# Cross-attention block: two query tiles' scores in one block, one ring of PSUM banks, exchanges gated by target, layer norms placed anew

## Chip, cores and metric

One core of one Trainium2 chip runs the whole kernel in one launch. The metric is the device time in microseconds (us) of that launch; lower is better. TensorE (PE) multiplies, VectorE (DVE) and ScalarE (ACT) work on its results, GpSimd (POOL) does small element work, and SyncE (SP) issues nearly all transfers from one in-order queue.

## What is computed

All in float32, for 4 batches of 512 queries and 512 keys, width 512, 16 heads of 32, inner width 2048:

```python
y = layer_norm(x) * ln1_w + ln1_b
q, k, v = y @ q_w + q_b, ctx @ k_w + k_b, ctx @ v_w + v_b      # 16 heads of 32
attn = softmax(where(mask, q @ k.T / sqrt(32), lowest))        # 512 x 512 per head
hidden = (attn @ v) @ cproj_w + cproj_b + x
z = layer_norm(hidden) * ln2_w + ln2_b
out = hidden + gelu_tanh(z @ fc_w + fc_b) @ proj_w + proj_b
```

## The kernel before

The work has two parts. In the first (to about 551 us) the attention of all batches runs, and the MLP of batch 0 and half of the MLP of batch 1 are filled in between; in the second, `last_mlps`, the rest of the MLPs runs. Instruction order on every engine is the order of the program text (a manual schedule), so each engine is a queue in that order.

The attention is cut into 16 `w` = (batch, group of 4 heads), each with 4 query tiles of 128 (`qt`): 64 units `u = 4w + qt`. Two units make a pair, numbered `2w + half`. One unit does this:

- `scores(w, qt)`: four matmuls, one for each head (L262). A head is only 32 rows deep, so the four lie side by side in four row strips of the array. They write the one tile of the pool `ps_sc`: `[128, 4, 512]`, four PSUM banks, one buffer. The other four banks are the pool `ps_acc`, which all other products take in turn (`acc_tile`).
- Then, head by head, DVE adds the mask and takes the row minimum (L266; the scores are negated), and ACT takes the exponential with its row sum (L270). This is called softening here.
- `turn(w, qt)`: DVE transposes 32 x 32 squares of two heads at a time into the pair's tile `tb` (L285, L293), with the reciprocals of the sums (L290, L292, L294). `tb` has two buffers.
- After a pair's second unit, `exchange()` and `copies` move `tb` across partition strips to the pair's target with 16 DMAs on SP's queue (L328): `pT` (one buffer), or the spare tile `gt` for pairs 1, 3, 5, 7, or `xe` for pairs 25, 27, 29, 31. A pair for `pT` waits in `waiting` while another pair is in `held`, and pairs behind it wait with it.
- `attend(w, half)`: 16 matmuls with four column strips (L345, tile `av`), multiplied by the reciprocals on DVE into `oT` (L350); only then is the target free. The table `AT` and `LAG` say in which unit a pair is attended: as a rule in the first unit of the block after next, at the beginning and the end of the attention in a second unit.

Between `scores` of one unit and the next, PE gets other work, from hand-written lists (`first`, `later`): the key, query and value products of later groups (`prep_k`, `prep_q`, `prep_v`: `acck`, `accq`, `accv`), the output product `cproj` (`accc`, four for a batch), the pairs of MLP products by a seven-product scheme (`fc_seven`, tiles `q...`), plain MLP products (`accf`) and the second MLP product (`accp`). Evictions of these go to ACT (K, Q, V, the copy `p1` and gelu of a pair) or DVE (sums into `h`, the adds of `fc_seven`).

A layer norm is `ln_stat` (DVE, L128 and L129, a tile of 128 rows each), `ln_rs` (POOL, L134 and L136, and two more for keys in `BY_ACT`, L140 and L141), `ln_norm` (DVE L150, or ACT L146 for keys in `BY_ACT`), and `ln_turn` (PE transposes, tile `tp`, scaled by ACT L164 or DVE L162). A key is (1 or 2, batch).

Of the kernel before, what the change touches and what calls it, by code (L numbers as in the profile page):

```python
# [12 lines left out]
F32 = mybir.dt.float32  # L13
# [20 lines left out]
AHEAD = 3  # L34
SPLIT = 1
FIRST = 2
LAG = 4
# [15 lines left out]
def xattn_block(ctx: ExitStack, tc: tile.TileContext, x, encT, mask, q_w, k_w, v_w, c_w, fc_w, p_w, vecs, rows, out):  # L53
# [3 lines left out]
    def pools(stack, **bufs):  # L57
        return [stack.enter_context(tc.tile_pool(name=n, bufs=k)) for n, k in bufs.items()]
# [3 lines left out]
    ps_acc = ctx.enter_context(tc.tile_pool(name="ps_acc", bufs=4, space=PSUM))  # L62
# [3 lines left out]
    ps_sc = att.enter_context(tc.tile_pool(name="ps_sc", bufs=1, space=PSUM))  # L66
# [53 lines left out]
    def acc_tile(name):  # L120
        return ps_acc.tile([P, D], F32, tag="acc", name=name)
# [9 lines left out]
    def ln_rs(key):  # L131

        ve = small.tile([P, NT], F32, tag="ve", name=f"ve{key[0]}_{key[1]}")
        nc.gpsimd.tensor_scalar(ve, S["mv", key][:, :, 1], EPS, 1.0, ALU.add, ALU.mult)  # L134
        rs = small.tile([P, NT], F32, tag="rs", name=f"rs{key[0]}_{key[1]}")
        nc.gpsimd.tensor_tensor(rs, ve, nhalf, ALU.pow)  # L136
        S["rs", key] = rs
        if key in BY_ACT:
            nm = small.tile([P, NT], F32, tag="nm", name=f"nm{key[0]}_{key[1]}")
            nc.gpsimd.tensor_tensor(nm, S["mv", key][:, :, 0], rs, ALU.mult)  # L140
            nc.gpsimd.tensor_scalar(nm, nm, -1.0, 0.0, ALU.mult, ALU.add)  # L141
            S["nm", key] = nm

    def ln_norm(key, t, dst, src):
        if key in BY_ACT:
            nc.scalar.activation(  # L146
                dst, src, AF.Identity, bias=S["nm", key][:, t : t + 1], scale=S["rs", key][:, t : t + 1]
            )
            return
        nc.vector.tensor_scalar(  # L150
            dst, src, S["mv", key][:, t, 0:1], S["rs", key][:, t : t + 1], ALU.subtract, ALU.mult
        )
# [102 lines left out]
    def scores(w, qt):  # L255
        if qt == 0:
            S["sums", w] = small.tile([P, NT, HG], F32, tag="sums", name=f"sums_{w}")
        qT, kT, sums = S["qT", w], S["kT", w], S["sums", w]
        sc = ps_sc.tile([P, HG, L], F32, tag="sc", name=f"sc_{w}_{qt}")
        for h in range(HG):  # L260
            r = slice(h * HD, (h + 1) * HD)
            nc.tensor.matmul(sc[:, h, :], qT[r, ts(qt, P)], kT[r, :], start=True, stop=True)  # L262
        for h in range(HG):
            s = score_tile()
            mn = small.tile([P, 1], F32, tag="mn", name=f"mn_{w}_{qt}_{h}")
            nc.vector.tensor_tensor_reduce(  # L266
                out=s, in0=sc[:, h, :], in1=S["mb", w // NG], scale=1.0, scalar=FMAX,
                op0=ALU.add, op1=ALU.min, accum_out=mn,
            )
            nc.scalar.activation(s, s, AF.Exp, bias=mn, scale=-1.0, accum_out=sums[:, qt, h : h + 1])  # L270
            if h % 2:
                S["ps", w, qt, h // 2] = score_pair()

    def turn(w, qt):

        half, q = divmod(qt, 2)
        if q == 0:


            S["tb", w, half] = two.tile([P, NI, PW + 2 * HD], F32, tag="tb", name=f"tb_{w}_{half}")  # L280
        tb = S["tb", w, half]
        tv = tb[:, :, :PW].rearrange("p j (a t h q) -> p a h t j q", a=2, t=NT, h=HG)
        two_heads = [(tv[:, q, 2 * k : 2 * k + 2], S["ps", w, qt, k]) for k in range(HG // 2)]
        for k in range(HG // 2 - q):
            nc.vector.transpose(*two_heads[k])  # L285
        if q == 0:
# [6 lines left out]
        nc.vector.transpose(*two_heads[-1])  # L293
        nc.vector.transpose(  # L294
            tb[:, :, PW:].rearrange("p j (a q) -> p a j q", a=2), rr.rearrange("p a h d -> p (a h d)")
        )
        waiting.append((w, half))
        if w < NW - 1 or half == 0:
            exchange()

    waiting, held = [], []

    def exchange():

        while waiting:
            w, half = waiting[0]
            if 2 * w + half not in IN_G + IN_XE:
                if held:
                    return
                held.append((w, half))  # L310
            waiting.pop(0)
            copies(w, half)

    def copies(w, half):
        tb = S["tb", w, half]

        pair = 2 * w + half
        if pair in IN_G or pair in IN_XE:
            pT = (gt if pair in IN_G else xe).rearrange("p (i n) -> p i n", i=NI)
        else:  # L320
            pT = one.tile([P, NI, PW + 2 * HD], F32, tag="pT", name=f"pT_{w}_{half}")
# [9 lines left out]
    def attend(w, half):  # L331
# [19 lines left out]
        if (w, half) in held:  # L351
            held.remove((w, half))
# [237 lines left out]
    def last_mlps():  # L590
        last, = pools(ctx, last=1)
        ps_last = ctx.enter_context(tc.tile_pool(name="ps_last", bufs=4, space=PSUM))
# [241 lines left out]
    def do(fn):  # L834
        return [(0.0, fn)]
# [60 lines left out]
    for part in range(3):  # L896
# [15 lines left out]
    first = [[] for _ in range(NW)]  # L912
    later = [[] for _ in range(NW)]
    k2, q2, v2 = A(2)
    k3, q3, v3 = A(3)
    k4, q4, v4 = A(4)
    k5, q5, v5 = A(5)
    k6, q6, v6 = A(6)
    first[0] = (
        [(CHAIN, lambda: prep_v(1))], [v2, k2] + x2[:1], [k3, (CHAIN, lambda: (prep_v(3), load_enc(1)))] + x2[1:2],  # L920
        [(CHAIN, lambda: prep_q(1))]
    )
    first[1] = [q2] + x2[2:], [k4], [v4], [q3]
    first[2] = x3[:2] + [k5], x3[2:], [v5], [q4]
    first[3] = [q5], [k6], [v6], [q6] + do(lambda: c_bias(0))
# [31 lines left out]
    def norm(b, *ts_):  # L957
        return do(lambda: [norm2(b, t) for t in ts_])


# [3 lines left out]
    first[4] = x1 + [k, q, v] + x4  # L964
    later[4] = c[:1] + x2[:1] + c[1:2] + x2[1:2] + c[2:3] + x2[2:] + c[3:]
    k, q, v = A(8)
    first[5] = (
        [k] + stat(0, 0, 1, 2, 3) + rs(0) + do(fc_sums) + x3 + norm(0, 0, 1, 2, 3) + [v], [q] + t2 + do(lambda: y_sums(0)), some(2) + pb_(0), some(2)
    )
    k, q, v = A(9)  # L970
    x1, x2, x3, x4 = inputs(3)
    first[6] = [k, q] + some(4) + [v] + x1
    k, q, v = A(10)
    first[7] = [k, q] + x2[:1] + some(2) + x2[1:2] + some(2) + [v]

    k, q, v = A(11)
    first[8] = h_(1, 0, 1) + x2[2:] + [k, q] + x3[:2] + some(2) + x3[2:3] + [v] + x3[3:] + h_(1, 2, 3) + x4
    later[8] = cb(1) + C(1)
    k, q, v = A(12)
    first[9] = [q] + some(2) + [k] + some(2) + [v]  # L980
    k, q, v = A(13)
    first[10] = [k, q] + some(4) + [v]
    k, q, v = A(14)
    t2 = turns2(1)
    first[11] = (
        [k, q] + stat(1, 0, 1, 2, 3) + rs(1), some(2) + norm(1, 0, 1, 2, 3), some(1) + t2[:2] + [v],
        t2[2:] + pb_(1) + some(1) + h_(2, 2, 3, 0, 1)
    )

    k, q, v = A(15)  # L990
    c = C(2)
    first[12] = [k, q], cb(2) + [v], c[:2], c[2:]
    first[13] = some(1), some(1) + stat(2, 0, 1), some(1) + stat(2, 2, 3) + rs(2), some(2)
    first[14] = some(1) + norm(2, 0, 1), some(1) + norm(2, 2, 3), some(2), some(1)
    first[15] = hid_(1, 2, 3) + some(1), some(1), some(1), some(2)

    for w in range(NW):
        if w and w % NG == 0:
            make_mb(w // NG)

        work, rest = first[w], later[w]
        by_unit = isinstance(work, tuple)
        share = 0 if by_unit else sum(c for c, _ in work + rest) / NT
        due = 0.0
        for qt in range(NT):
            u = w * NT + qt
            pair = AT.get(u, (u - LAG) // 2 if u >= LAG and u % 2 == 0 else None)
            if pair in AT.values() and u not in AT:
                pair = None
            if pair is not None:  # L1010
                attend(*divmod(pair, 2))
            scores(w, qt)
            turn(w, qt)
            if by_unit:
                run(work[qt])
                continue

            if qt == 2:
                work, rest = work + rest, []
            due += share / 2  # L1020
            due -= run(work, due)
            due += share / 2
            due -= run(work, due)
        if not by_unit:
            run(work + rest)
# [5 lines left out]
    run(some(2))  # L1031
    attend(NW - 1, 0)
    run(some(2))
    load_wa(first_c)
    run(some(2))
    p_sums(first_c)
    attend(NW - 1, 1)
    run(mlp)
# [52 lines left out]
```

## Time and profile before

| | |
|---|---|
| time, median of 3 runs | 797.86 us (797.24 to 799.24) |
| span of the profiled execution, first to last instruction | 795.4 us |
| median less that span, which is what lies around the span if the profiled execution was like the median run | 2.4 us |
| busy share of the span: PE, DVE, ACT, POOL | 98%, 78%, 43%, 18% |
| attention part, to the first product of `last_mlps` | about 551 us |
| mean granted TensorE clock | 0.998 |

The profile names instructions by line, engine, operation and tiles (`out<-in`). A float32 matmul leaves two records, a transpose on PE one, so `sc L262 x8` is one unit's four score matmuls. In the chain of waits and in the timeline the first number is the start in us from the span's beginning and the second the length. SP's queue only issues: its rows are the time of issuing, and a transfer lands later.

### The profile page before, as it was taken

The page shows a single profiled execution, that of the slowest core. Times are in us where ns is not written, and L with a number is a line of the kernel's source. Part 1 is how long each engine was busy: PE and PEld are TensorE (multiplying, and loading weights), DVE is VectorE, ACT ScalarE, POOL GpSimd, SP SyncE. Part 2 cuts the span into 40 slices and gives each one's busy share as a digit, 9 for nine tenths or more (in the row PEclk, how much of TensorE's full clock was granted, in tenths as well). Part 3 has the DMA queues.
Part 4 walks back from the last instruction along what each step waited for, and adds up shares of the span by engine and source line. Part 5 has one row for each costly group of instructions (what it writes and reads, how often), then busy time and mean ns, then how long its engine had stood idle before and what let it go on. Part 6 is the DMA issues. An engine that isn't in the chain of part 4 may idle for free.

```text
span 795.4 us, 12670 instructions
## 1 busy us (share of the span) xinstructions
PE 779.7 (98%) x4394; PEld 502.0 (63%) x4394; DVE 622.0 (78%) x1256; ACT 341.9 (43%) x754; POOL 145.4 (18%) x161
## 2 busy tenths in 40 slices
PE   9999999989999999999999999999999999999998
PEld 6545445456655555555654333445888889988897
DVE  3789988888789866878878997635887999779863
ACT  2567766447763545546643469700210321012200
POOL 1210021055120041101131000120041004400052
PEclk9999999999999999999999999999999999999999
DMA  9899999947897877788668799873442330022001
GB/s 335 280 237 235 225 234 239 246 115 180 209 242 172 244 205 192 162 199 220 165 166 221 177 273 227 221 248 134 159 159 88 93 122 17 27 80 81 14 14 40
DMA packets 60959, 137.19 MB, mean 172 GB/s; under 512 B 12464, under 2 KB 15664, under 8 KB 60768
## 3 DMA queue, kind: packets, MB, share of 16 engines
q1 hardware_dynamic: 59472, 132.43, 61.3%
q0 software_dynamic: 896, 2.82, 1.0%
q10 hardware_dynamic: 528, 1.14, 0.7%
q8 instruction: 35, 0.57, 0.3%
q14 instruction: 28, 0.23, 0.1%
HBM read 58.22 MB, written 6.82 MB: 82 GB/s over the span
## 4 chain that ended last, share of the span: by engine, by line
PE 85%; DVE 5%; SPq 5%; DMA 1%; issue 1%; ACT 1%; POOL 0%; DVEq 0%; POOLq 0%; ACTq 0%
PE q L495 20%; PE accp L554 8%; PE r L642 7%; PE sc L262 7%; PE accc L386 7%; PE av L345 7%; PE accv L240 7%; PE acck L218 6%; SPq L328 5%; PE accq L228 5%; PE accf L536 3%; DVE ptt L266 2%; PE q4p L679 2%; PE q1p L697 2%; PE tp L159 1%; PE q2p L679 1%
## 5 line engine op out<-in xcount | busy, mean ns | idle before, releaser
L270 ACT ACTIVATE ptt<-ptt,mn 128x512 f32<-128x512 f32 x256 | 181.6, 710 | 136.1 <-DVE mn L266 135.8
L266 DVE CUSTOM_DVE_ANT_0 ptt<-sc,mb 128x512 f32<-128x512 f32 x256 | 161.0, 685 | 33.3 <-PE sc L262 33.0
L285 DVE STREAM_TRANSPOSE tb<-ptt 128x1024 f32<-128x1024 f32 x96 | 119.2, 1242 | 14.4 <-ACT ptt L270 12.9
L554 PE MATMUL accp<-pbt,gt 128*128 128x512 f32 x192 | 86.7, 600 | 0.0
L495 PE MATMUL q<-yT,gt 128*128 128x256 f32 x320 | 78.9, 379 | 0.0
L262 PE MATMUL sc<-pbt 32*128 32x512 f32 x512 | 73.0, 640 | 4.7 <-DVE mn L266 2.5
L513 ACT ACTIVATE ga<-ga,vec 128x512 f32<-128x512 f32 x40 | 26.7, 714 | 95.7 <-DVE ga L455 95.7
L495 PEld LDWEIGHTS q<-yT,gt 128*128 128x128 f32 x320 | 60.8, 190 | 8.7 <-issue 0.5
L554 PEld LDWEIGHTS accp<-pbt,gt 128*128 128x128 f32 x192 | 35.2, 190 | 49.0 <-issue 45.8
L240 PEld LDWEIGHTS accv<-ptt,xe 128*128 128x128 f32 x512 | 58.7, 192 | 9.5 <-issue 6.7
L495 PE MATMUL q<-ys,gt 128*128 128x256 f32 x240 | 61.8, 380 | 0.5 <-DVE ys L452 0.5
L240 PE MATMUL accv<-ptt,xe 128*128 128x128 f32 x512 | 60.8, 277 | 0.0
L218 PE MATMUL acck<-xe,ptt 128*128 128x512 f32 x128 | 59.3, 606 | 0.0
L228 PE MATMUL accq<-xe,ptt 128*128 128x512 f32 x128 | 58.4, 599 | 0.0
L386 PE MATMUL accc<-wc,oT 128*128 128x512 f32 x128 | 56.6, 596 | 0.0
L252 POOL TENSOR_TENSOR v<-v,row 128x512 f32<-128x512 f32 x16 | 20.4, 1275 | 172.9 <-ACT v L245 172.9
L345 PE MATMUL av<-pT,v 128*32 128x256 f32 x768 | 48.0, 392 | 2.7 <-DMA ptt<-v_w_dram 0.8
L495 PEld LDWEIGHTS q<-ys,gt 128*128 128x128 f32 x240 | 45.4, 190 | 7.4 <-DVE ys L452 0.9
L270 ACT ACTIVATION_READ_ACCUMULATOR ptt<-ptt,mn 128x1 f32 x256 | 47.8, 187 | 0.0
L228 PEld LDWEIGHTS accq<-xe,ptt 128*128 128x128 f32 x128 | 23.6, 190 | 32.4 <-issue 30.4
L262 PEld LDWEIGHTS sc<-pbt 32*128 32x128 f32 x512 | 20.0, 183 | 37.9 <-issue 21.5
L386 PEld LDWEIGHTS accc<-wc,oT 128*128 128x128 f32 x128 | 23.8, 190 | 31.5 <-issue 29.8
(180 smaller groups left out, 1141.3 us busy)
## 6 DMA issues: line engine op xcount, KB each, us to landing
pT<-tb SPq DMA_DIRECT2D x384, 136.0 KB, 2.4
pbt<-p_w_dram SPq DMA_DIRECT2D x40, 256.0 KB, 3.2
gt<-fc_w_dram SPq DMA_DIRECT2D x40, 256.0 KB, 2.6
gt<-tb SPq DMA_DIRECT2D x64, 136.0 KB, 2.7
xe<-tb SPq DMA_DIRECT2D x56, 136.0 KB, 3.6
pbt<-fc_w_dram SPq DMA_DIRECT2D x24, 256.0 KB, 4.0
ptt<-k_w_dram SPq DMA_DIRECT2D x16, 256.0 KB, 3.8
xe<-encT_dram SPq DMA_DIRECT2D x16, 256.0 KB, 5.4
```

The lines of the kernel that those rows point to most:

```text
L218: nc.tensor.matmul(acc, S["wk", w][:, d, :], eT[:, d, :], start=(d == 0), stop=(d == ND - 1))
L228: nc.tensor.matmul(acc, S["wq", w][:, d, :], xT[:, d, :], start=(d == 0), stop=(d == ND - 1))
L240: nc.tensor.matmul(acc[:, ts(t, P)], eT[:, d, ts(t, P)], S["wv", w][:, d, :], start=(d == 0), stop=(d == ND - 1),)
L262: nc.tensor.matmul(sc[:, h, :], qT[r, ts(qt, P)], kT[r, :], start=True, stop=True)
L266: nc.vector.tensor_tensor_reduce(out=s, in0=sc[:, h, :], in1=S["mb", w // NG], scale=1.0, scalar=FMAX, op0=ALU.add, op1=ALU.min, accum_out=mn,
L270: nc.scalar.activation(s, s, AF.Exp, bias=mn, scale=-1.0, accum_out=sums[:, qt, h : h + 1])
L285: nc.vector.transpose(*two_heads[k])
L345: nc.tensor.matmul(av[ts(h, HD), : 2 * P].rearrange(shape, **kw), v[:, t, ts(h, HD)], p[t][h], start=(t == 0), stop=(t == NT - 1),)
L386: nc.tensor.matmul(acc, S["oT", b][:, g, ts(t, P)], wc[:, g, :], start=(g == 0), stop=(g == NG - 1))
L495: nc.tensor.matmul(o, x[:, k], y[:, k], start=(k == 0), stop=(k == 1))
L554: nc.tensor.matmul(acc, gT[q % 2][:, k, ts(t, P)], S["pw", b, q * FQ + k], start=(k == 0), stop=(k == FQ - 1))
L642: nc.tensor.matmul(r, x[:, c], w[:, c], start=(c == 0), stop=(c == NP // 2 - 1))
```

## The change

Eight score matmuls, of two query tiles, now stand back to back. `scores` takes a bank of its own for each head, from one ring of eight banks (`ps_att`) that every product of the attention part uses in turn; `ps_acc` and `ps_last` open only in `last_mlps`. A `block` (there are 32, one for each pair) softens all eight heads, transposes, and has three places for other work, `fill(0)`, `fill(1)`, `fill(2)`. The first two take work up to one product's cost each, the third the rest. Pair `p` is attended at the start of block `p + 2` from block 10 on, `p + 3` in blocks 3 to 8, and block 9 attends pairs 6 and 7. An exchange is issued when its own target is free. The normalisation of key (2, 0) moves from DVE to ACT and stands ahead of block 10, and its statistics move into block 9. Those of batch 2's second layer norm move from units 53 to 57 behind the attention.

```diff
-AT = {u: (u - 5) // 2 for u in (5, 7, 9, 11, 13, 15, 17, 19, 53, 55, 57, 59, 61, 63)}
 BY_ACT = ((1, 1), (1, 2))
+NORM_ACT = BY_ACT + ((2, 0),)
...
-    ps_acc = ctx.enter_context(tc.tile_pool(name="ps_acc", bufs=4, space=PSUM))
-    ps_sc = att.enter_context(tc.tile_pool(name="ps_sc", bufs=1, space=PSUM))
+    banks = [att.enter_context(tc.tile_pool(name="ps_att", bufs=8, space=PSUM))]
...
     def acc_tile(name):
-        return ps_acc.tile([P, D], F32, tag="acc", name=name)
+        return banks[-1].tile([P, D], F32, tag="acc", name=name)
...
     def scores(w, qt):
...
-        sc = ps_sc.tile([P, HG, L], F32, tag="sc", name=f"sc_{w}_{qt}")
+        S["sc", w, qt] = [acc_tile(f"sc_{w}_{qt}_{h}") for h in range(HG)]
         for h in range(HG):
             r = slice(h * HD, (h + 1) * HD)
-            nc.tensor.matmul(sc[:, h, :], qT[r, ts(qt, P)], kT[r, :], start=True, stop=True)
+            nc.tensor.matmul(S["sc", w, qt][h], qT[r, ts(qt, P)], kT[r, :], start=True, stop=True)
...
+    def block(w, half, fill):
+
+        q0, q1 = 2 * half, 2 * half + 1
...
+        scores(w, q0)
+        scores(w, q1)
+        soften(w, q0, 0, 1, 2, 3)
+        soften(w, q1, 0, 1)
+        turn(w, q0, 0)
+        soften(w, q1, 2, 3)
+        fill(0)
+        turn(w, q0, 1)
         rs = small.tile([P, 2, HG], F32, tag="rsum", name=f"rsum_{w}_{half}")
         nc.vector.reciprocal(rs, S["sums", w][:, 2 * half : 2 * half + 2, :])
         rr = one.tile([P, 2, HG, HD], F32, tag="rr", name=f"rr_{w}_{half}")
         nc.scalar.copy(rr, rs[:, :, :, None].broadcast_to([P, 2, HG, HD]))
-        nc.vector.transpose(*two_heads[-1])
+        turn(w, q1, 0)
+        fill(1)
+        turn(w, q1, 1)
         nc.vector.transpose(
             tb[:, :, PW:].rearrange("p j (a q) -> p a j q", a=2), rr.rearrange("p a h d -> p (a h d)")
         )
         waiting.append((w, half))
         if w < NW - 1 or half == 0:
             exchange()
+        fill(2)
...
-        while waiting:
-            w, half = waiting[0]
-            if 2 * w + half not in IN_G + IN_XE:
-                if held:
-                    return
-                held.append((w, half))
-            waiting.pop(0)
+        while waiting and target(*waiting[0]) not in held:
+            w, half = waiting.pop(0)
+            held[target(w, half)] = w, half
             copies(w, half)
...
+    put(9, c[:1], x2[1:2], c[1:2], x2[2:], stat(0, 0), c[2:3], stat(0, 1), c[3:], stat(0, 2, 3), rs(0))
...
+    put(10, [k], do(fc_sums), x3, [v], t2, do(lambda: y_sums(0)), [q], before=norm(0, 0, 1, 2, 3))
+    put(11, some(2), pb_(0), some(2))
...
+    put(22, [k, q], stat(1, 0, 1, 2, 3), rs(1), some(2), norm(1, 0, 1, 2, 3))
...
+    due = {p: (p - 2,) for p in range(10, 2 * NW)}
+    due |= {p: (p - 3,) for p in range(3, 9)} | {9: (6, 7)}
+    for p in range(2 * NW):
...
+        run(ahead[p])
+        for pair in due.get(p, ()):
+            attend(*divmod(pair, 2))
+
+        def fill(n, work=fills[p]):
+            run(work, CHAIN if n < 2 else None)
+
+        block(w, half, fill)
```

Apart from that, four normalisations move from DVE to ACT, POOL gets two instructions more, and ACT loads its function tables 22 times instead of 30; the other instructions and the bytes moved stay as they were. In the built program each of the 256 score matmuls now signals on its own and 252 of them carry a wait for their bank, where before one matmul of four waited and one signalled.

More of the change, by code (lines that the diff above doesn't have):

```diff
@@ L144, in ln_norm @@
     def ln_norm(key, t, dst, src):
[L145 removed]
+        if key in NORM_ACT:
             nc.scalar.activation(
@@ L268, in scores, with turn @@
                 op0=ALU.add, op1=ALU.min, accum_out=mn,
             )
-            nc.scalar.activation(s, s, AF.Exp, bias=mn, scale=-1.0, accum_out=sums[:, qt, h : h + 1])
+            nc.scalar.activation(s, s, AF.Exp, bias=mn, scale=-1.0, accum_out=S["sums", w][:, qt, h : h + 1])
             if h % 2:
                 S["ps", w, qt, h // 2] = score_pair()
[L274 to L281, printed above, removed]
-        tv = tb[:, :, :PW].rearrange("p j (a t h q) -> p a h t j q", a=2, t=NT, h=HG)
[L283 to L286, printed above, removed]
-            return
+    def turn(w, qt, k):
+        tb = S["tb", w, qt // 2]
+        tv = tb[:, :, :PW].rearrange("p j (a t h q) -> p a h t j q", a=2, t=NT, h=HG)
+        nc.vector.transpose(tv[:, qt % 2, 2 * k : 2 * k + 2], S["ps", w, qt, k])
@@ L350, in attend @@
         nc.vector.tensor_tensor(o, a, r, ALU.mult)
-        if (w, half) in held:
-            held.remove((w, half))
+        del held[target(w, half)]
         exchange()
@@ L909, in xattn_block @@
     v_bias(0)
[L912 to L925, printed above, removed]
     mlp = []
@@ L958, in norm, with put @@
         return do(lambda: [norm2(b, t) for t in ts_])
+    ahead, fills = {}, {}
+    def put(p, *work, before=()):
+        work = [item for part in work for item in part]
+        ahead[p] = list(before)
+        fills[p] = work
+    k2, q2, v2 = A(2)
+    k3, q3, v3 = A(3)
+    k4, q4, v4 = A(4)
+    k5, q5, v5 = A(5)
+    k6, q6, v6 = A(6)
+    put(0, [(CHAIN, lambda: prep_v(1)), v2, k2], x2[:1])
+    put(1, [k3, (0.0, lambda: prep_q(1)), (CHAIN, lambda: (prep_v(3), load_enc(1)))], x2[1:2])
+    put(2, [q2], x2[2:], [k4])
+    put(3, [q3, v4])
+    put(4, x3[:2], [k5], x3[2:])
+    put(5, [v5, q4])
+    put(6, [q5, k6])
+    put(7, [v6, q6], cb(0))
     x1, x2, x3, x4 = inputs(2)
@@ L979, in xattn_block @@
+    put(17, [v], x3[3:], h_(1, 2, 3), x4, cb(1), C(1))
     k, q, v = A(12)
-    first[9] = [q] + some(2) + [k] + some(2) + [v]
+    put(18, [q], some(2), [k])
+    put(19, some(2), [v])
     k, q, v = A(13)
-    first[10] = [k, q] + some(4) + [v]
+    put(20, [k, q], some(2))
+    put(21, some(2), [v])
     k, q, v = A(14)
     t2 = turns2(1)
[L985 to L988, printed above, removed]
+    put(22, [k, q], stat(1, 0, 1, 2, 3), rs(1), some(2), norm(1, 0, 1, 2, 3))
@@ L990, in xattn_block @@
+    put(23, some(1), [v], t2, pb_(1), some(1), h_(2, 2, 3, 0, 1))
     k, q, v = A(15)
     c = C(2)
[L992 to L998, printed above, removed]
-            make_mb(w // NG)
[L1001 to L1025, printed above, removed]
@@ new lines, in xattn_block @@
+    put(24, [k, q], cb(2), [v])
+    put(25, c)
+    put(26, some(2))
+    put(27, some(3))
+    put(28, some(3))
+    put(29, some(3))
+    put(30, hid_(1, 2, 3), some(3))
+    put(31, some(3))
+    due = {p: (p - 2,) for p in range(10, 2 * NW)}
+    due |= {p: (p - 3,) for p in range(3, 9)} | {9: (6, 7)}
+    for p in range(2 * NW):
+        w, half = divmod(p, 2)
+        if half == 0 and w and w % NG == 0:
+            make_mb(w // NG)
+        run(ahead[p])
[4 more added lines that the diff above has]
+        block(w, half, fill)
@@ L1030, in xattn_block @@
     c_bias(B - 1)
-    run(some(2))
+    run(some(1) + stat(2, 0, 1))
     attend(NW - 1, 0)
-    run(some(2))
     load_wa(first_c)
-    run(some(2))
+    run(some(1) + stat(2, 2, 3) + rs(2) + some(1) + norm(2, 0, 1) + some(1))
+    attend(NW - 1, 1)
+    run(mlp + norm(2, 2, 3))
     p_sums(first_c)
-    attend(NW - 1, 1)
-    run(mlp)
     load_wa(first_c + 1)
```

49 lines of the change are left out of this document (24 added, 25 removed).

## Prediction

> **What bounds the kernel now.** I read the page first: span, busy shares, chain.
>
> ```profile
> span 795.4 us, 12670 instructions
> PE 779.7 (98%) x4394; PEld 502.0 (63%) x4394; DVE 622.0 (78%) x1256; ACT 341.9 (43%) x754; POOL 145.4 (18%) x161
> PE 85%; DVE 5%; SPq 5%; DMA 1%; issue 1%; ACT 1%; POOL 0%; DVEq 0%; POOLq 0%; ACTq 0%
> ```
>
> PE is the chain for 85%. So only two things can shorten the run: PE's own work, or its few idle stretches. The windows view gives the idle time by stage (length of the stretch less PE busy), and the PE timeline shows the worst place.
>
> ```profile
> 174.00:178.00 4.00, 4.00 (x40) 1.57 (x32) 2.42 (x4) 0.41 (x1) 2.55 (x2) 0.60 0.00 0
> 178.00:195.00 17.00, 16.30 (x108) 12.04 (x104) 14.33 (x29) 11.97 (x24) 11.10 (x13) 1.00 0.77 194
> 195.00:430.00 235.00, 233.80 (x1320) 129.11 (x1312) 188.09 (x395) 130.87 (x296) 38.66 (x43) 1.00 0.78 196
> 430.00:550.00 120.00, 118.84 (x559) 49.53 (x559) 86.94 (x182) 59.66 (x123) 11.67 (x13) 1.00 0.81 224
> ...
> 172.94 0.65 PE L159 MATMUL tp<-ident,xn 128*128 128x128 f32 x4 [3.06 <-ACT pbt L231]
> 173.61 3.51 PE L345 MATMUL av<-pT,v 128*32 128x256 f32 x32
> 330.82 1.93 PE L345 MATMUL av<-pT,v 128*32 128x256 f32 x32
> ```
>
> From 178 to 550 us PE idles only 0.70 + 1.20 + 1.16 = 3.1 us. The one large hole is the second layer norm of batch 0 at 170 us: 3.06 us idle, and right behind it the granted clock is 0.60 for 4 us, so that an `av` takes 3.51 instead of 1.93. Together 3.06 + 1.58 = 4.6 us. The rest is PE at work, so the gain must come from the work's form. The chain shows that:
>
> ```profile
> 415.04 7.06 PE accc L386 x16
> 422.10 1.07 PE sc L262 x8
> 423.17 7.07 PE accc L386 x16
> 430.24 1.07 PE sc L262 x8
> ...
> 537.59 13.75 PE accc L386 x32
> ...
> 153.85 1.11 PE sc L262 x8
> ...
> 327.32 3.57 PE accv L240 x32
> ```
>
> 32 records of `accc` in one piece take 13.75, 0.43 each; in two pieces, each behind a `sc`, 7.06 + 7.07 = 14.13, so 0.19 more for each entry. A `sc` is two passes of that length, 0.86, but takes 1.07: 0.21 more. Each change between full-array and strip matmuls costs about 0.2 us.
>
> **The change, part by part.**
>
> *Scores back to back.* A block's order was `av`, `sc`, work, `sc`, work: five such changes. It becomes `av`, `sc sc`, work: three. That is 0.19 + 0.21 = 0.40 us in each block in which PE sets the pace, if two `sc` follow each other without a gap. The trace has no such pair. Nearest rows: sixteen products of `av` at the same tiling run in 1.93, of which eight steps of 0.215 (half of 0.43) are 1.72, so steps within one tiling join without a gap; the other bound is a full 0.21. I take 0, by the `av` row.
>
> Each score matmul now waits for its own bank and signals by itself. The MLP products do that all along:
>
> ```profile
> 698.77 48.35 PE q L495 x224
> ```
>
> 0.2158 us per record, 256 columns at full rate, although their tiles wait and signal: nothing, then. [...]
>
> *One ring of eight banks.* Eight scores fill the ring, so the next product, `fill(0)`, takes the bank of the first score and waits until DVE has softened it. Before, the next product had its own banks, and only the next `sc`, one unit later, waited for DVE. DVE's steps:
>
> ```profile
> 154.99 0.69 DVE L266 CUSTOM_DVE_ANT_0 ptt<-sc,mb 128x512 f32<-128x512 f32 x1 [0.65 <-PE sc L262]
> 155.60 0.69 DVE L266 CUSTOM_DVE_ANT_0 ptt<-sc,mb 128x512 f32<-128x512 f32 x1
> 157.44 2.49 DVE L285 STREAM_TRANSPOSE tb<-ptt 128x1024 f32<-128x1024 f32 x2
> 159.85 0.65 DVE L128 BATCH_NORM_STATS2 st<-h 128x6 f32<-128x512 f32 x1
> 160.64 0.66 DVE L128 BATCH_NORM_STATS2 st<-h 128x6 f32<-128x512 f32 x1
> 164.51 3.54 DVE L150 TENSOR_SCALAR xn<-h,mv,rs 128x512 f32<-128x512 f32 x4 [1.41 <-POOL rs L136]
> 171.78 1.19 DVE L293 STREAM_TRANSPOSE tb<-ptt 128x1024 f32<-128x1024 f32 x1
> 172.90 0.40 DVE L294 STREAM_TRANSPOSE tb<-rr 128x256 f32<-128x256 f32 x1
> 177.17 0.42 DVE L350 TENSOR_TENSOR oT<-av,pT 128x256 f32<-128x256 f32 x1 [1.07 <-PE av L345]
> ```
>
> One head costs 0.61 (start to start), a transpose 1.25, a statistics tile 0.79, four normalisations 3.54. A softening starts some 1.15 us after its `sc` (153.85 to 154.99) and takes 0.69, so it frees its bank at 1.85 to 1.95 with the signal; PE comes out of two `sc` at 4 x 0.43 + 0.2 = 1.92. So with DVE idle at the block's start the wait costs 0 to 0.1; with DVE late, every microsecond is one of PE. A block of DVE is 8 x 0.61 + 4 x 1.25 + 0.4 + 0.42 = 10.7 us plus what its fills bring. **A block therefore lasts as long as the longer of PE's work and DVE's.** PE's is 1.72 (two `sc`) + 1.72 (`av`) + 3 x 0.2 + 3.44 for each K, Q, `accc` or `accp` (3.57 for V, 28 x 0.216 = 6.05 for an MLP pair). Queued behind a waiting `fill(0)` on PE is all the rest of the block, so nobody else fills the gap.
>
> Blocks 0 to 8 hold two or three products (10.9 us with two) against DVE's 10.7. But here the exchange sets the pace:
>
> ```profile
> 63.45 10.91 SPq L328 DMA_DIRECT2D pT<-tb  x16
> 122.06 11.10 SPq L328 DMA_DIRECT2D gt<-tb  x16
> 318.44 10.18 SPq L328 DMA_DIRECT2D pT<-tb  x16
> 333.27 10.63 SPq L328 DMA_DIRECT2D pT<-tb  x16
> 345.82 1.93 PE L345 MATMUL av<-pT,v 128*32 128x256 f32 x32 [0.23 <-DMA pT<-tb]
> ```
>
> Pairs 2 to 7 leave SP's queue back to back, one each (122.06 - 63.45)/5 = 11.7 us, weights between them. In the changed order the loads ahead of pair 1 still wait for `accv_3` at the end of block 1, so that pair starts near 50 as before, and with two `tb` buffers the blocks run at SP's 11.7. Pair 7, issued until 133.2, lands near 135; block 9 now attends it at its start, half a block earlier than before. So PE waits there for what it was ahead, some 3 us, and by block 10 nothing is won: **0**, with -3 to +3 as ends.
>
> From block 10 (154 us, the same work done in both) to 551 us:
>
> - 22 blocks x 0.40 = **-8.8**. The old hole and the idle time: **-4.6 - 3.1**.
> - Block 10, the norm on ACT, ahead of the block's exponentials. By my count its statistics end about 1 us into block 10, since the last output product's sum and two statistics tiles come behind block 9's last product. Then POOL, then four normalisations:
>
> ```profile
> 144.79 0.20 POOL L134 TENSOR_SCALAR ve<-mv 128x4 f32<-128x4 f32 x1 [8.46 <-DVE mv L129]
> 146.47 0.19 POOL L141 TENSOR_SCALAR nm<-nm 128x4 f32<-128x4 f32 x1
> 168.69 0.72 ACT L270 ACTIVATE ptt<-ptt,mn 128x512 f32<-128x512 f32 x1 [4.20 <-DVE mn L266]
> 169.41 0.71 ACT L270 ACTIVATE ptt<-ptt,mn 128x512 f32<-128x512 f32 x1
> L146 ACT ACTIVATE xn<-xn,nm,rs 128x512 f32<-128x512 f32 x8 | 5.8, 801 | 0.0
> ```
>
>   POOL 1.9, ACT 4 x 0.80 = 3.2: the exponentials (0.71 apart) start 6.1 into the block instead of 1.9. The evictions behind them on ACT (K, four `tp`) come 4.2 later, and the second norm's transposes find their ring banks still full: PE loses about **+2.0**, though not the 4.6.
> - An MLP pair in `fill(0)` or `fill(1)`: its copy `p1` now stands on ACT behind eight exponentials (the last softening ends 1.15 + 8 x 0.61 + 1.25 = 7.3 us into the block, the last exponential near 8.3), and DVE's four adds behind it (0.69 + 0.66 + 0.42 + 0.69 = 2.5).
>
> ```profile
> L455 DVE TENSOR_TENSOR gt<-q,gt 128x512 f32<-128x512 f32 x16 | 11.1, 692 | 3.0 <-PE q L495 1.5
> L455 DVE TENSOR_TENSOR gt<-q,p 128x512 f32<-128x512 f32 x8 | 5.3, 657 | 0.7 <-PE q L495 0.7
> L455 DVE TENSOR_TENSOR gt<-gt 128x256 f32<-128x256 f32 x20 | 8.4, 420 | 7.2 <-DMA gt<-fc_w_dram 7.1
> ```
>
>   Block 11 (two pairs): DVE 17.3 against PE 16.1, **+1.2**. Blocks 13 and 21 (a pair and V): 14.7 against 13.7, **+1.0 each**.
> - Block 22 brings four statistics, a pair's adds and four normalisations on DVE: 10.7 + 3.2 + 2.5 + 3.5 = 19.9 against PE's 17.0, **+2.9**. Before, DVE could run this late behind the next unit's work.
> - Block 26 has two `accp` only (10.9): DVE 10.7 + 2 x 0.66, **+1.2**. Block 16: its transposes wait for norms on DVE, **+0.5**.
> - Blocks with 14.5 us of PE (15, 19, 24, and 27 behind the short 26) touch the exchange's own round: from `av` at 330.82 to the next at 345.82 are 15.0 us, of which 10.63 issuing. About **+0.3** for three, **+0.9** for 27.
> - The bare wait of `fill(0)`, 22 x 0.07: **+1.5**.
>
> Sum: -16.5 + 13.1 = -3.4. The tail (`last_mlps`, 245 us) has the same products; the statistics moved behind the attention lie beside 45 us of PE work with DVE free, 0. So the span goes from 795.4 to 792.0; with the 2.4 us by which the median lies above the span, **794.5 us**.
>
> **The rivals.**
>
> *DVE late everywhere (slower).* My blocks assume that DVE reaches the next softening in time. If bank waits, ACT's lateness or the transposes' wait on exponentials cost it just 0.6 us a block more than I counted, 22 x 0.6 = 13.2 go onto the path: 807.7. It decides from 0.15 us a block (3.4/22). For it: 78% DVE busy, 188.09 of 235 us in the middle stage, and a slack that shrinks from most of a unit to 0.05 us. Against: in 12 of the 22 blocks PE's work exceeds DVE's by 2 us or more. Chance 0.26.
>
> *The layout fits better than I cost it.* The four items above one microsecond (blocks 10, 11, 22, 26: 7.3 us) and the exchange floors vanish, because POOL or ACT are earlier than I place them: about 784. For it: ACT is at 43% and loads fewer tables. Chance 0.16.
>
> *The exchange is the clock (no change).* If the round of 15 us binds wherever PE falls below 15, half the 8.8 is not collected: about 798. For it: the 0.23 us wait at 345.82. Chance 0.12.
>
> [...] Chance 0.06.
>
> *The clock.* The wait for pair 7 is as long as the idle time that went ahead of the 0.60. If the clock halves again, 1.6 more: 796.1, within my forecast's own range. [...]
>
> **The numbers.** Forecast 794.5, chance 0.40, own range 789 to 799 (early part -3 to +3, `sc sc` gap up to 22 x 0.21 = 4.6 late); of it 0.34 is faster by over 0.3% (below 795.5, about what a measurement of this kernel tells from no change) and 0.06 within. Faster: 0.34 + 0.16 = 0.50. Same: 0.06 + 0.12 + 0.06 = 0.24. Slower: 0.26. The range runs from the better layout, 784, to the slower rival, 807.
>
> **What would show it.** Right: `sc x16` at about 1.92 to its successor; no 0.60 clock at 170 us; block 9 starting at 135 to 138 us behind pair 7's landing; `fill(0)` products waiting for DVE in blocks 11, 13, 21 and 23, most in 23 (about 3 us). Wrong: `sc x16` at 2.1 or more; PE waiting for softening in every block; or hardly any in 23.

## The result, and the profile after

The changed kernel takes **801.17 us** (median of four runs, 800.17 to 803.88), beside 797.55 us for the kernel before: a ratio of **1.0055**, 95% interval 1.0031 to 1.0078. It is slower by 0.55%. The forecast was 794.5, with 789 to 799 as its own range: the time lies above that range, and the sign was wrong. It lies inside the wide range over all rivals, 784 to 807, but only because VectorE being late everywhere had stretched that one upwards, and that is not what happened; this is luck. The profiled execution took 800.17 us with a span of 798.2, 2.8 us more than the 795.4 of before, and these 2.8 us are what the traces have to explain.

The page of after: span, busy time, and the chain that ended last.

```profile
span 798.2 us, 12709 instructions
PE 779.3 (98%) x4394; PEld 514.0 (64%) x4394; DVE 614.2 (77%) x1252; ACT 331.7 (42%) x750; POOL 145.1 (18%) x163
PE 74%; SPq 10%; DVE 9%; DMA 2%; issue 2%; ACT 2%; DVEq 0%; ACTq 0%
```

PE is as busy as before, but the chain runs through it for 74% instead of 85%: DVE and SP's queue now set the end in places. The windows view says in which (length, then busy time and instructions of PE, PEld, DVE, ACT, POOL, then granted clock, DMA share, GB/s):

```profile
116.00:137.00 21.00, 18.37 (x134) 10.15 (x136) 13.76 (x31) 7.90 (x20) 7.11 (x7) 0.96 0.88 239
...
155.00:181.00 26.00, 22.52 (x144) 14.09 (x136) 15.16 (x32) 14.62 (x30) 11.52 (x15) 0.87 0.46 117
181.00:434.00 253.00, 249.90 (x1460) 146.80 (x1456) 200.97 (x426) 139.00 (x318) 49.70 (x56) 1.00 0.77 199
434.00:465.00 31.00, 27.96 (x152) 11.79 (x148) 24.81 (x55) 12.55 (x35) 1.62 (x3) 1.00 0.82 225
```

PE idles 2.6 us before the scores of block 9, 3.5 us in block 10 (155 to 181, with a clock of 0.87), 3.1 us in blocks 11 to 25 together, and 3.0 us in block 27. PE's timeline at those places:

```profile
134.18 2.59 PE L348 MATMUL av<-gt,v 128*32 128x256 f32 x32 [2.49 <-DMA gt<-tb]
...
161.44 1.91 PE L156 MATMUL tp<-ident,xn 128*128 128x128 f32 x16
163.19 3.74 PE L237 MATMUL accv<-ptt,xe 128*128 128x128 f32 x32
169.75 1.94 PE L156 MATMUL tp<-ident,xn 128*128 128x128 f32 x8 [2.83 <-DVE mn L263]
172.34 2.09 PE L156 MATMUL tp<-ident,xn 128*128 128x128 f32 x8 [0.65 <-ACT pbt L217]
174.22 4.62 PE L225 MATMUL accq<-xe,ptt 128*128 128x512 f32 x8
...
444.57 3.15 PE L257 MATMUL sc<-pbt 32*128 32x512 f32 x16
447.65 10.57 PE L556 MATMUL accp<-pbt,gt 128*128 128x512 f32 x24
461.23 1.93 PE L348 MATMUL av<-pT,v 128*32 128x256 f32 x32 [3.01 <-DMA xe<-tb]
```

The hole of the second layer norm is still there, at the same place as before: 3.5 us of waiting in two pieces, and a half clock behind it (0.50 from 169.44 to 176.27). At the half clock the second sixteen `tp` take 1.94 + 2.09 = 4.03 us, where the first sixteen took 1.91, and an `accq` of 3.6 us takes 4.62: 3.1 us more for the same work. The row at 461.23 names `xe<-tb`, a transfer of the next exchange; what its products read is pair 26, whose last transfer landed at 460.66. What made the hole of block 10 is seen on ACT, with POOL's and DVE's rows beside it:

```profile
157.88 0.19 POOL L138 TENSOR_SCALAR nm<-nm 128x4 f32<-128x4 f32 x1
...
163.14 2.93 ACT L143 ACTIVATE xn<-h,nm,rs 128x512 f32<-128x512 f32 x4 [10.82 <-PE tp L156]
165.98 0.71 ACT L267 ACTIVATE ptt<-ptt,mn 128x512 f32<-128x512 f32 x1
...
167.51 1.25 DVE L275 STREAM_TRANSPOSE tb<-ptt 128x1024 f32<-128x1024 f32 x1 [7.06 <-ACT ptt L267]
```

POOL had the statistics ready at 158.07. The four normalisations waited until 163.14, and the releaser is PE's `tp`: they write new tiles of the pool `tiles` (tag `xn`, four buffers), whose last holders are batch 2's rows, and those are read by the transposes that stand in `fill(1)` of the same block. The exponentials, queued behind on ACT, began 10.6 us into the block; DVE's transposes waited 7.06 us for them; and PE ran out of work. Block 10 lasted 25.23 us.

### The profile page after: what moved, and what is told of

The parts are those of the page before. It is cut to its first block, busy times and chain, and to the rows that moved or that the text cites. A ratio compares the mean times of both kernels' runs of the same rounds, so it can differ in the third digit from the quotient of the medians.

```text
span 798.2 us, 12709 instructions
## 1 busy us (share of the span) xinstructions
PE 779.3 (98%) x4394; PEld 514.0 (64%) x4394; DVE 614.2 (77%) x1252; ACT 331.7 (42%) x750; POOL 145.1 (18%) x163
## 2 busy tenths in 40 slices
DMA packets 60960, 137.20 MB, mean 172 GB/s; under 512 B 12464, under 2 KB 15664, under 8 KB 60768
## 4 chain that ended last, share of the span: by engine, by line
PE 74%; SPq 10%; DVE 9%; DMA 2%; issue 2%; ACT 2%; DVEq 0%; ACTq 0%
PE q L497 17%; SPq L331 9%; PE accp L556 9%; PE r L645 7%; PE accc L388 7%; PE av L348 6%; PE sc L257 6%; PE acck L215 5%; PE accq L225 4%; PE accf L538 3%; PE accv L237 3%; DVE ptt L263 3%; PE q4p L682 2%; DVE tb L275 2%; PE tp L156 1%
## 5 line engine op out<-in xcount | busy, mean ns | idle before, releaser
L275 DVE STREAM_TRANSPOSE tb<-ptt 128x1024 f32<-128x1024 f32 x128 | 154.7, 1220 | 10.8 <-ACT ptt L267 8.7
L348 PE MATMUL av<-pT,v 128*32 128x256 f32 x768 | 46.4, 382 | 5.7 <-DMA xe<-tb 3.0
L257 PEld LDWEIGHTS sc<-pbt 32*128 32x128 f32 x512 | 28.6, 188 | 34.7 <-issue 20.0
```

What stands on the lines that cost most here:

```text
L257: nc.tensor.matmul(S["sc", w, qt][h], qT[r, ts(qt, P)], kT[r, :], start=True, stop=True)
L275: nc.vector.transpose(tv[:, qt % 2, 2 * k : 2 * k + 2], S["ps", w, qt, k])
L348: nc.tensor.matmul(av[ts(h, HD), : 2 * P].rearrange(shape, **kw), v[:, t, ts(h, HD)], p[t][h], start=(t == 0), stop=(t == NT - 1),)
```

## The experiments

Times are medians; ratios are to the kernel before, run beside each, with their 95% interval. "Block 10" is the distance from its first score to the next block's.

| kernel | time, us | ratio | block 10, us |
|---|---|---|---|
| changed kernel | 801.17 | 1.0055 (1.0031 to 1.0078) | 25.23 |
| norm_own | 796.77 | 0.9977 (0.9953 to 1.0) | 19.06 |
| norm_late | 796.03 | 0.9965 (0.9946 to 0.9984) | 18.53 |
| av7_later | 805.25 | 1.0095 (1.0067 to 1.0123) | 25.67 |
| sc_apart | 811.53 | 1.0167 (1.0141 to 1.0192) | 25.94 |
| b26_late | 790.13 | 0.9899 (0.988 to 0.9919) | 18.52 |
| w_act | 801.71 | 1.0054 (1.0036 to 1.0071) | 18.36 |
| act21_late | 792.97 | 0.9938 (0.9913 to 0.9962) | 18.52 |
| all1 | 795.69 | 0.9975 (0.9962 to 0.9989) | 18.32 |
| best1 | 789.17 | 0.9891 (0.9874 to 0.9909) | 18.52 |
| best_fill | 792.83 | 0.9935 (0.9916 to 0.9954) | 18.52 |
| best_fill4 | 789.99 | 0.9888 (0.9864 to 0.9913) | 18.32 |
| best_early | 788.09 | 0.9875 (0.9858 to 0.9893) | 18.36 |

One kernel's runs differ by up to 9 us here (norm_late 791.73 to 798.04, norm_own 790.49 to 799.61), and block 10 starts between 154 and 162 us in the profiled ones. So block lengths are compared inside the traces, and times by the ratios.

**Was it the tile pool, or POOL?**

```diff
 # norm_own
-        y = tiles.tile([P, D], F32, tag="xn", name=f"xn2_{b}_{t}") if stays(b, t) else h
+        y = gT[1][:, t] if b == 0 else tiles.tile([P, D], F32, tag="xn", name=f"xn2_{b}_{t}") if stays(b, t) else h
 # norm_late
-    put(10, [k], do(fc_sums), x3, [v], t2, do(lambda: y_sums(0)), [q], before=norm(0, 0, 1, 2, 3))
+    put(10, [k], do(fc_sums), x3, norm(0, 0, 1, 2, 3), [v], [q], t2, do(lambda: y_sums(0)))
```

> The four normalised tiles of batch 0 get a place of their own (the second half of gt, free at that time) instead of the tile pool in which batch 2's rows still wait for their transposes; order unchanged. My theory (the norms waited for that pool, not for POOL's statistics): they start when POOL's nm is there, near 2.7 us into block 10 instead of 7.7, the exponentials near 6 us instead of 10.6; block 10 lasts 20 to 21 us instead of 25.2, no half clock in it, the time is near 796.7. Rival 1 (norms ahead of the exponentials cost this wherever they stand, POOL being the late one): block 10 stays above 24 and the time above 800. Rival 2 (VectorE is late everywhere and eats what one block wins): block 10 is shorter by 4 to 5 us, the time by less than 1.5.

> The same four norms, still on ScalarE and in the same tile pool, but put behind batch 2's transposes in block 10, with V and Q ahead of batch 0's own transposes. My theory: the exponentials start at once (1.9 us into the block), the pool is free when the norms come, block 10 lasts 19 to 20.5 us, no half clock, the time is near 796 (795 to 797.5). Rival 1 (POOL late): no difference to the former kernel, since POOL has been ready for long by then; so norm_late would be far faster than norm_own, 796 against 800. Rival 2 (VectorE late everywhere): 800.

ACT's timeline, first norm_own, then norm_late:

```profile
160.61 2.93 ACT L143 ACTIVATE gt<-h,nm,rs 128x512 f32<-128x512 f32 x4 [5.79 <-POOL nm L138]
163.45 0.71 ACT L267 ACTIVATE ptt<-ptt,mn 128x512 f32<-128x512 f32 x1
```

```profile
157.19 0.72 ACT L267 ACTIVATE ptt<-ptt,mn 128x512 f32<-128x512 f32 x1 [5.12 <-DVE mn L263]
...
167.20 2.94 ACT L143 ACTIVATE xn<-h,nm,rs 128x512 f32<-128x512 f32 x4
170.02 0.59 ACT L242 COPY v<-accv 128x512 f32<-128x512 f32 x1
```

With tiles of their own the norms start when POOL is done, 2.7 us into the block, the exponentials at 5.6, and block 10 is 6.2 us shorter with no half clock in it (1.00 from 157.9 to 176.9). Placed behind the transposes, the exponentials start at 2.1 us and the block is 6.7 us shorter. Both times came out as the theory had them (796.7 and 796). The waiting buffer is shown as the cause: 25.23 less 18.53 is 6.7 us, and the waiting of 3.5 and the half clock's 3.1 account for nearly all of it. With the waiting buffer gone the ratio is 0.9965, and the forecast's 794.5 against 797.86 would be 0.9958, within the interval of norm_late (0.9946 to 0.9984). The price of standing ahead of the exponentials, once the buffer is free, is about 0.5 us (19.06 less 18.53, with V and Q in another order too).

**Is the back-to-back order worth what it was said to be?**

```diff
         scores(w, q0)
-        scores(w, q1)
         soften(w, q0, 0, 1, 2, 3)
+        fill(0)
+        scores(w, q1)
         soften(w, q1, 0, 1)
         turn(w, q0, 0)
         soften(w, q1, 2, 3)
-        fill(0)
```

> Only the back-to-back order of the scores is undone: the first piece of work of a block stands between the two score products again (ring of eight banks, layout and exchanges as in the changed kernel). My theory: each block pays 0.40 us again, 8.8 us over the 22 blocks from block 10 on, and saves the waits for the softening, some 5 us by the trace: 805 (803 to 809). Rival (VectorE late everywhere because eight scores fill the ring): the waits saved are more than the tiling changes cost, the time is below 800. If the tiling changes cost nothing: 796.

PE's timeline at the start of block 19, in the changed kernel and then in sc_apart:

```profile
319.86 2.00 PE L257 MATMUL sc<-pbt 32*128 32x512 f32 x16
321.79 7.13 PE L556 MATMUL accp<-pbt,gt 128*128 128x512 f32 x16
```

```profile
328.16 1.14 PE L257 MATMUL sc<-pbt 32*128 32x512 f32 x8
329.23 3.70 PE L556 MATMUL accp<-pbt,gt 128*128 128x512 f32 x8
332.86 1.14 PE L257 MATMUL sc<-pbt 32*128 32x512 f32 x8
333.93 1.55 PE L556 MATMUL accp<-pbt,gt 128*128 128x512 f32 x3
```

Two scores and two pieces take 1.93 + 6.97 = 8.90 us back to back (321.79 less 319.86; 328.76, where the next product starts, less 321.79). Apart, score, piece, score take 1.07 + 3.63 + 1.07 up to 333.93, and a second piece of 3.63 would make 9.40: 0.5 for a pair of 0.40 forecast. Whole blocks give a cleaner number: in the eight blocks in which neither trace shows a wait (11, 18, 20, 24, 25, 26, 29, 30) sc_apart takes 0.40 to 0.41 us longer each, for instance 11.27 against 10.86 in block 26. That is the forecast 0.40. From block 11 to block 31 sc_apart loses 5.2 us on the changed kernel (it is 7.4 us behind at the one, 12.65 at the other), not 20 x 0.40 = 8.0, mainly since waits of the changed kernel fall away in it: block 12, without its 1.35 us, is 0.95 shorter. The rival of a VectorE that is late everywhere would have made this kernel the faster one; it is slower by about 9 us (1.0167 against 1.0055), more than my 4. The 7.4 us before block 11 I had not expected: pair 1's exchange starts at 54.65 instead of 50.71, everything behind it on SP's queue shifts, PE waits 6.15 us for pair 7, and the `av` behind that wait takes 3.56 us instead of 1.93. The edit also puts the first piece's evictions ahead of the second tile's softening, so the 9 us are not the price of the order alone.

**The wait for pair 7.**

```diff
 # av7_later, on the changed kernel
-    put(9, c[:1], x2[1:2], c[1:2], x2[2:], stat(0, 0), ...
+    put(9, c[:1], x2[1:2], c[1:2], do(lambda: attend(3, 1)), x2[2:], stat(0, 0), ...
-    due |= {p: (p - 3,) for p in range(3, 9)} | {9: (6, 7)}
+    due |= {p: (p - 3,) for p in range(3, 9)} | {9: (6,)}
```

> The attention products of pair 7 move from the start of block 9 to behind the second output product in it, so TensorE has 8 us of work while that exchange lands. The wait of 2.87 us and the half clock behind it (1.7 us) fall away in block 9. My theory: SyncE's queue is busy without a break up to 150 us, pair 8 lands at 152.1 whatever TensorE does, so block 10 can start at most 1.4 us earlier (154.0 instead of 155.4); the time is near 800 (799.5 to 801). Rival (the wait and the clock are the whole loss of this stage): block 10 starts 4 us earlier and the time is near 797.

Both missed: it is slower. DVE's timeline:

```profile
136.73 0.69 DVE L125 BATCH_NORM_STATS2 st<-xn 128x6 f32<-128x512 f32 x1 [6.70 <-DMA xn<-x_dram]
...
138.66 0.68 DVE L263 CUSTOM_DVE_ANT_0 ptt<-sc,mb 128x512 f32<-128x512 f32 x1
```

Block 9's scores now stood at 132.2, but DVE was blocked on the statistics of batch 2's rows. These are loaded behind pair 7's exchange on the same queue. The wait for pair 7 had hidden the wait for the rows; PE now idled 4.61 us, and the clock fell to 0.54.

```diff
 # w_act, on norm_late; the same for K and Q
-        load_w(w + 2, names=("wv",))
         nc.scalar.copy(v, acc.rearrange("p (t f) -> p t f", t=NT))
         S["v", w] = v
+        load_w(w + 2, side(w), ("wv",))   # nc.scalar for w in 2 to 6
```

> norm_late, and the K, Q and V weights loaded in blocks 1 to 8 are issued on ScalarE's queue, behind the eviction that follows the same product, instead of SyncE's, which has no break there from 44 to 150 us. Thirteen loads at some 0.45 us each between pairs 1 and 7. My theory (SyncE's issuing is the pace up to block 9): pair 7 lands 4 to 5 us earlier, near 129, TensorE does not wait 2.9 us for it, no half clock in block 9, block 10 starts near 152 instead of 155, the time is 792.5 (791 to 794.5). Rival 1 (the 16 DMA engines themselves are full there, at a share of 0.88 to 1.0): pair 7 lands as before, 796. Rival 2 (another load on the same queue, such as batch 2's rows, becomes the last): the wait for pair 7 goes but VectorE waits for the rows, 795 to 798.

SP's queue, first in norm_late, then in w_act, in which nothing stands between the exchanges any more:

```profile
62.72 10.82 SPq L331 DMA_DIRECT2D pT<-tb  x16
...
97.56 10.54 SPq L331 DMA_DIRECT2D gt<-tb  x16
```

```profile
65.02 12.53 SPq L334 DMA_DIRECT2D pT<-tb  x16
...
101.95 12.56 SPq L334 DMA_DIRECT2D gt<-tb  x16
114.61 13.44 SPq L334 DMA_DIRECT2D pT<-tb  x16
```

It missed: 801.71 for 792.5. Rival 1 holds, and more: with the weights beside them the exchanges take 2 us longer each on the mean (pairs 2 to 6: 12.5 against 10.6), and pair 7 lands at 140.08 instead of 133.60. Between 62 and 118 us the DMA engines' share is 0.90 in norm_late and 0.88 here, and they moved 233 and 216 GB/s: a second issuing queue brought no more through. `all1` carried this edit too and lost what the others won:

> The four edits together (norms behind the transposes, third piece in block 26, weights on ScalarE's queue, batch 1's norms on ScalarE). If each wins what my theory says and none hides another: 796.0 - 4 - 3.5 - 1.2 = 787. If VectorE's lateness or the exchange set a floor behind them: 792 or more.

It took 795.69 for the 787 expected, 6.5 more than best1, which differs from it in this edit alone.

**The short block, and the norms of batch 1** (both on norm_late).

```diff
 # b26_late
-    put(26, some(2))
+    put(26, some(3))
...
-    put(31, some(3))
+    put(31, some(2))
 # act21_late
-    NORM_ACT = BY_ACT + ((2, 0),)
+    NORM_ACT = BY_ACT + ((2, 0), (2, 1))
```

> norm_late, and the short block 26 gets a third output piece (three accp instead of two), which block 31 gives up. My theory: in the changed kernel pair 26's transposes end 1.7 us into block 27, its exchange lands when block 27's work is over by 3.0 us, and block 27's first product waits 1.15 us for VectorE; with 3.4 us more work in block 26 both waits go: 796.0 - 4 = 792 (791 to 793.5), block 27 near 14.3 us instead of 18.3. Rival (the exchange's round sets the pace of these blocks): the wait comes back in the next block, the time stays at 795 to 796.

> norm_late, and the four normalisations of batch 1 in block 22 go to ScalarE as well. My theory: VectorE reaches block 23's softening in time, the wait of 1.3 us of its first product for a bank goes: 794.8. Rival (ScalarE then delivers the exponentials or the normalised tiles later, and the transposes wait for them): 796 or more.

PE in block 27 of b26_late, against 444.57 to 461.23 of the changed kernel above:

```profile
443.70 2.00 PE L257 MATMUL sc<-pbt 32*128 32x512 f32 x16
445.63 10.57 PE L556 MATMUL accp<-pbt,gt 128*128 128x512 f32 x24
456.41 1.93 PE L348 MATMUL av<-pT,v 128*32 128x256 f32 x32 [0.21 <-DVE tb L298]
```

Both waits are gone: block 27 takes 14.57 us instead of 18.52 (18.34 in norm_late, on which this kernel is built), and blocks 26 and 27 together 28.86 instead of 29.38 (29.19 in norm_late) with one more piece of 3.43 in them. The ratio fell from 0.9965 to 0.9899, 5.3 us for the 4 expected; the intervals allow both. act21_late's ratio is 0.9938, about 2 us for the 1.2 expected, again within the intervals. Block 23, in the changed kernel and then in act21_late:

```profile
384.09 1.99 PE L257 MATMUL sc<-pbt 32*128 32x512 f32 x14
386.26 1.12 PE L257 MATMUL sc<-pbt 32*128 32x512 f32 x2 [0.18 <-DVE oT L353]
387.31 3.70 PE L556 MATMUL accp<-pbt,gt 128*128 128x512 f32 x8
```

```profile
376.73 2.00 PE L257 MATMUL sc<-pbt 32*128 32x512 f32 x16
378.66 3.70 PE L556 MATMUL accp<-pbt,gt 128*128 128x512 f32 x8
```

3.22 us against 1.93: the 1.3 us that was expected of this edit (norm_late has 3.24 there). The wait sits one step earlier than the prediction put it. The ring's bank that the eighth score takes is that of the `av` just before, and it is free only when DVE, behind its queue, has multiplied it into `oT`.

**All that won, and what holds the early part.**

> The three edits that each won: the norms behind the transposes, the third piece in block 26, batch 1's norms on ScalarE; the weights stay on SyncE's queue. If they add up (790.1 with the first two, 1.3 us for the wait in block 23): 788.8 (787.5 to 790).

It took 789.17, inside the range: the three edits add up.

```diff
 # best_fill; best_fill4 has range(4)
         for pair in due.get(p, ()):
+            if pair == 7:
+                idle = acc_tile("idle")
+                for _ in range(8):
+                    nc.tensor.matmul(idle, ident, row[:, 0, :], start=True, stop=True)
             attend(*divmod(pair, 2))
```

> best1, and eight products of no use (identity by a constant row, 3.4 us of TensorE) stand ahead of pair 7's attention products in block 9, where TensorE waits near 2.9 us. My theory (an idle stretch of about 3 us halves the granted clock for the next 3.4 us, which costs 1.7): the wait is filled, no half clock in block 9, 1.2 to 1.7 us less than best1. Rival (the clock falls for another reason, or pair 8 sets the start of block 10 anyway): the same time as best1, or 0.5 more.

> best_fill with four products of no use instead of eight: a product took 0.89 us there, not 0.43, so eight held TensorE 3.1 us past pair 7's landing; four take 3.6 us, as long as the wait. Theory: no half clock in block 9 and no time lost to the filler, 789.2 - 1.6 = 787.6 (786.5 to 788.8). Rival (pair 8's landing sets the start of block 10): as best1, 789.2.

PE's timeline around pair 7 in best1, in best_fill and in best_fill4:

```profile
136.73 3.57 PE L348 MATMUL av<-gt,v 128*32 128x256 f32 x32 [4.17 <-DMA gt<-tb]
```

```profile
131.01 7.13 PE L1023 MATMUL idle<-row,ident 128*128 128x512 f32 x16
138.08 1.93 PE L348 MATMUL av<-gt,v 128*32 128x256 f32 x32
```

```profile
130.54 3.70 PE L1023 MATMUL idle<-row,ident 128*128 128x512 f32 x8
134.69 1.93 PE L348 MATMUL av<-gt,v 128*32 128x256 f32 x32 [0.45 <-issue]
...
153.59 1.93 PE L348 MATMUL av<-pT,v 128*32 128x256 f32 x32 [0.56 <-DMA pT<-tb]
```

With the stretch filled, the clock stays at 1.00 (from 120 to 180 us in both fillers, where best1 has 0.50 from 136.7 to 138) and `av` takes 1.93 instead of 3.57: the idle stretch is what halved the clock here. The time does not show the 1.6 us: best_fill4 has 0.9888 and best1 0.9891, and intervals of 1.4 to 2 us to each side cannot tell 1.6 from nothing, so the times leave the rival open. The traces say more. From pair 7's landing to block 10's first score they show 21.5 us in best1 (136.43 to 157.96), in the changed kernel and in norm_late, and 21.1 in best_fill4 (134.39 to 155.45). Only some 0.5 of the 1.6 is left: 0.56 goes to a wait for pair 8, which landed at 153.24, and about 0.5 to block 9's scores, which take 2.46 us instead of 1.93. The rival holds in part. Eight products took 7.1 us, twice what I meant, and held PE 3.1 us past the landing. The last kernel takes the wait away by order alone:

```diff
 # best_early, on best1: av7_later's edits, and
-    put(7, [v6, q6], cb(0))
+    put(7, x1, [v6, q6], cb(0))
-    put(8, x1, [k, q, v], x2[:1], x4)
+    put(8, [k, q, v], x2[:1])
-    put(9, ..., stat(0, 2, 3), rs(0))
+    put(9, ..., stat(0, 2, 3), rs(0), x4)
```

> best1, and the wait for pair 7 taken away by order alone: pair 7's products behind the second output product of block 9, batch 2's rows loaded ahead of pair 7's exchange (block 7's work) so that VectorE does not wait for them as it did in av7_later, batch 2's encoder loads behind pair 8's exchange. My theory: pair 8 lands 2.5 to 3 us earlier, no half clock in block 9, block 10 starts at 151 to 152.5 instead of 155, the time is 785.5 (784.5 to 787.5). Rival (the 16 DMA engines, not the order on the queue, set when pair 8 lands): 788 to 790. Rival 2 (the encoder rows come too late for block 10's K): 788 or more.

The clock stays full in block 9 (1.00 from 130 to 155 us), and in the trace block 10 starts at 154.12, against 157.96 in best1; but the six kernels with the same program up to block 9's end start it anywhere from 155.12 (norm_late) to 157.96. The ratio moves only from 0.9891 to 0.9875, inside the intervals, and 788.09 us is outside the 784.5 to 787.5 expected and inside the first rival's range. PE's timeline in best_early:

```profile
147.76 4.56 PE L388 MATMUL accc<-wc,oT 128*128 128x512 f32 x10 [1.80 <-DVE oT L353]
152.25 1.93 PE L348 MATMUL av<-pT,v 128*32 128x256 f32 x32
```

PE waits 1.80 us for pair 7's product to be multiplied into `oT`, and pair 8 lands at 151.77, 0.48 us before its `av`: the transfers are still close behind. So best_early at 788.09 us, 1.25% below the kernel before, is the fastest here, and not by a measured distance from best1.

## Why the prediction was wrong, by its own steps

- **Block 10, +2.0 forecast: the step that failed.** I let the norms wait for statistics and POOL alone, and POOL was even a little earlier than I counted (2.7 us into the block for 2.9). I did not ask where they write. The destination tiles were held by batch 2's rows until the transposes of the same block, so a step put ahead of the block waited for a step inside it. The exponentials began 10.6 us into the block instead of 6.1, and the term of 2.0 us measured 6.7 (25.23 against norm_late's 18.53); the old hole, whose 4.6 us I had counted as won, stayed, with a clock of 0.56 between 169 and 173 us. By my terms block 10 and the old hole stood for -2.9 us against the kernel before (from the start of block 10 to that of block 11); it was 25.23 against 23.28, +1.95. norm_late starts its block 11 at 173.65 against 177.06 of before, -3.4, close to my -2.9, but partly by chance: its block 10 starts 1.3 us later than before's and is 4.75 us shorter, and its trace is of its fastest execution.
- **The early part, 0 with -3 to +3:** +1.6 us at the start of block 10. The mechanism was right (pair 7 landed at 133.88, PE waited, the clock was 0.50 from 135.3 to 138.7), but I priced the half clock at 1.6 us and left it out of the sum. That the transfers set the pace here is supported by w_act, where pair 7 landed 6.5 us later than in norm_late and block 10 began 5.4 later, and by best_fill4, where a full clock wins 0.5 us.
- **Block 27, +0.9:** 3.0 us for pair 26. Its transposes ended 1.7 us into block 27, since DVE was late in the short block 26, and the exchange's 11.2 us and a landing of 3.2 came on top. The step used one round of 15.0 us and did not start it from the transposes' end.
- **Mis-sized to the other side:** block 22 +2.9, measured 1.3 (blocks 22 and 23); blocks 13 and 21 +1.0 each, measured 0.4 and 0.3 among the next block's scores, besides 0.7 and 0.8 of waiting for exchanges, of which I had counted none there. Blocks 11 to 25 in all came out 2.1 us better than before, for the same work (by the first scores they last 253.1 in both, but before attended pair 24 only behind block 26's first score); by my terms (-6.0 for the tiling, -1.9 of idle time, +8.5 of waits) they were 0.6 worse.
- **Right:** the 0.40 us a block for the tiling (0.40 to 0.41 in sc_apart's blocks without a wait); two scores join without a gap (1.93 to the successor in blocks without a wait, so no run shows a price for the scores' own signals, the rival to which the prediction gave a chance of 0.06); block 11 +1.2, measured 1.35 among block 12's scores; block 26 +1.2, measured 1.15 among block 27's; the tail 0 (243.9 us against 244.0).

Of the 6.2 us between -3.4 and +2.8, block 10 is 4.9, the early part 1.6, the blocks from 26 on 2.5 (-1.1 forecast, +1.4 measured), and blocks 11 to 25 give 2.7 back. The rival that ended slower, VectorE late everywhere, was not what happened: sc_apart relieved VectorE and lost.

## What to carry to other kernels

When a step is moved ahead, list the buffers that it writes as well as the values that it reads: an engine's queue that stands still on a pool's last reader holds everything behind it, however early its inputs are (in block 10 the norms stood on ACT from 158.07, when POOL was done, to 163.14, and the exponentials behind them). A wait for one transfer can hide the next one on the same queue (in av7_later DVE stood 6.70 us for the rows behind pair 7's exchange), so read the landing of what is queued behind it before you remove it. And after a short block, start the exchange's clock from the end of the transposes, not from the block's.

## What the runs showed of the hardware

- How long PE idled just before did not decide by itself whether a half clock followed. In the changed kernel PE waited 2.49 us in front of pair 7, the granted clock was 0.50 from 135.31 to 138.72, and the `av` took 2.59 us instead of 1.93; it waited 3.01 us in front of pair 26, the clock was 1.00 from 461.2 to 464.5, and the `av` took 1.93. In front of pair 26 norm_late waited 2.83 us and its `av` took 1.93 too, but norm_own waited 3.08 (3.42 for the `av`, clock 0.53) and av7_later 3.02 (3.64). What separates these cases was not tested. That the idle time in front of pair 7 is what halved the clock there is shown by best_fill and best_fill4: filled with products, the clock stayed at 1.00 and the `av` took 1.93 us, where best1, with 4.17 us of waiting, has 3.57.
- Weight loads moved to a second queue (w_act against norm_late) lengthened the issuing of five exchanges on the first, from between 10.0 and 10.9 us to between 11.0 and 13.4, for the same bytes in all (137.20 MB).
